# Third experts: VectorE in written order, routing of the last block and the second list in parts, block totals ahead of a tile's own work

## The chip, the cores and the metric

The kernel runs on one core of one Trainium2 chip. The metric is the device time of one execution in microseconds (us), the median of three runs: 3441.6 us (3441.32 to 3441.97).

Engine names in the profile: PE is TensorE's matrix products, PEld its weight loads, DVE is VectorE, ACT is ScalarE, POOL is GpSimd, SP is SyncE, which here issues most transfers.

## The reference, cut to what matters

The program is a network of four stages on 4096 tokens of 256 channels. The first three (two convolution-like attentions, and a linear attention with a first layer of experts) are not touched by the change. The last stage is a full attention over all 4096 tokens, and then a layer of eight experts, of which each token uses two:

```python
# layer 3 (t: 4096 tokens x 256 channels, float32)
t = t + attention(layer_norm(t))
xf = layer_norm(t)
gate_logits = xf @ Wg + bg                      # 8 experts
top_w, top_i = top_k(gate_logits, 2); top_w = softmax(top_w)
for e in range(8):
    h = gelu(xf @ W1[e] + b1[e])                # 256 -> 1024
    out = out + w_dense[:, e] * (h @ W2[e] + b2[e])   # 1024 -> 256
t = t + out
x = channels_first(t)
```

## The kernel before

**Tokens and blocks.** The 4096 tokens are held as 32 tiles of 128 tokens (`NT`), in eight blocks of 512 (`NBLK`, four tiles `TPB` each). The attention goes block by block. While it works on the values of block b, the tokens of block b - 1 are finished (`finish`, L2769: projection, division by the softmax sum, addition to `t`) and routed.

**Routing (`route_parts`, L2034).** For a block: statistics and layer norm (`stats`, `root`, `scales`, `norm`), two turns into channel-first form (`turn`), the gate's logits, the two best experts (`top`, whose Exp runs on ScalarE, then `weigh`), a running count per expert (`count`), places in the experts' lists (`place` on TensorE, `find` on VectorE) and `scatter`: eight indirect DMAs that GpSimd issues, each writing 128 token rows of 260 numbers into the DRAM table `xs`. `route` (L2023) groups these parts into five steps. All of them that need PSUM take it through `bank()`, which after the attention is a single bank named "q".

**Lists of tiles (`list_tiles`, L2120).** The experts' work is cut into tiles of 256 token rows of one expert (`MT`). A table says for each tile its expert and where its rows begin. List "A" has `FULL` = 20 tiles that are already full from blocks 0 to 6, so it is made during the attention of the last block; list "B" holds what is left (19 tiles, of which the last three lie inside a run-time branch, L2326, that tests how many are used). `list_tiles` is a generator of two parts: many small VectorE operations, then a product that spreads the table over partitions.

**Expert tiles (`expert_tiles`, L2329).** Tile numbers run from 0 to 35. For tile i the loop does, in this order of text: SP loads the rows of tile i + 4 (`expert_rows`, L2269) and the weights of tile i + 2 (two transfers, L2276 and L2278; three sets of buffers); `first` (L2360): eight groups of products with gelu on ScalarE (L2367), PSUM pairs in three buffers; `sides` (L2388, L2396): four weight differences on GpSimd; `turn` of the rows of tile i + 1 (L2298: four transposes, one VectorE copy, L2302); `where` for tile i + 1 (L2281: eight or nine tiny VectorE operations that work out target rows and gate weights); then `second` for the tile before, i - 1. `second` calls `seven` (L2399): the second layer in seven products of 2x2 blocks instead of eight, which needs four half sums `hs` of `h` on VectorE (L2403 to L2406), the weight differences, and a combining of the products (L2420 to L2425); then bias (L2431), scaling by the gate weight on ScalarE (L2438) and two indirect DMAs on GpSimd that write the result rows to the DRAM table `ys` (L2439).

**The last block's routing and list B** are put between these tiles: `step()` in `expert_tiles` calls one of five routing steps and then the two parts of list B, one or two per tile, in tiles 0 to 3. The four `finish` of the last block come ahead of tile 0 and after each of its first three pairs of products (`ahead`).

**Block totals.** A block of 512 tokens can be summed when no later tile holds one of its rows. `read(b)` (L2859) loads the two result rows of each token from `ys` (two transfers, L2496); `give(b)` (L2863) adds both to `t` on VectorE (L2867, 128 x 1024 each), turns the block with transposes (L251) into PSUM bank "q", copies it out, the first half on ScalarE (L254), the second on VectorE (L256), and `send` writes it to the output. Blocks 0 to 5 are read in tiles 29 to 34, each beside `second`, and given one tile later; block 6 is read after tile 35's `first`, ahead of the last `second`; block 7 after the branch. Blocks 6 and 7 are summed by TensorE during their transposes, after everything else. A read of `ys` waits for the result scatters that stand before it in the text, and a scatter that stands after it waits for the read.

**What sets the order.** By default a planner orders each engine's instructions by estimates of costs and of when inputs are ready. Inside `tc.manual_schedule(engines=...)` the named engines keep the order of the text. Before the change, the experts have TensorE in written order only until the last `step` (tile 3); VectorE, ScalarE, GpSimd and SP are the planner's. In the attention loop of the last blocks TensorE and GpSimd are in written order. `limits3` (L2895) tests for the attention's number range with some nine small VectorE operations; its result is used at the very end.

Of the kernel before, what the change touches and what calls it, by code (L numbers as in the profile page):

```python
# [19 lines left out]
P = 128  # L20
# [72 lines left out]
class Net:  # L93
# [2026 lines left out]
    def list_tiles(self, S, wp, bank, nm, n):  # L2120
# [25 lines left out]
        nc.vector.tensor_sub(new, have, had)  # L2146
        ends = tl(NBLK * NE, "ends")[:, :K]
# [8 lines left out]
        if not whole:  # L2156
            nc.vector.tensor_copy(S["used"], ends[:, K - 1 : K])
            last = tl(1, "last")
            nc.vector.tensor_scalar_add(last, ends[:, K - 1 : K], -1.0)
            i = tl(1, "i")  # L2160
            nc.vector.tensor_tensor(i, self.nth[:, 0:1], last, ALU.min)
        at = tl(1, "pair")
# [5 lines left out]
        nc.vector.tensor_mul(pick, pick, had)  # L2168
        k = tl(1, "k")
# [135 lines left out]
    def experts(self, S, steps=None, pre=None):  # L2305

        tc = self.tc
        early = steps is not None
# [4 lines left out]
        def some(tiles, steps=(), pre=None):  # L2313
            with (
# [3 lines left out]
            ):  # L2318
                if pre:
                    order.enter_context(tc.manual_schedule(engines={mybir.EngineType.PE}))  # L2320
                self.expert_tiles(S, tiles, wp, ps, list(steps), early, pre, order)

        some(tiles, steps or (), pre)
# [5 lines left out]
    def expert_tiles(self, S, order, wp, ps, steps, early, pre, written):  # L2329
# [25 lines left out]

        def turn(x):
# [3 lines left out]
        def first(xT, w1, between=None):  # L2360
# [8 lines left out]
            for m in range(0, KH, 2):  # L2369
                p = ps.tile([P, 2, MT], F32, tag="h", name="f_h_ps", bufs=3)  # L2370
                if between is None:
# [3 lines left out]
                else:  # L2375
                    products(m, p)
                    products(m + 1, p)
                    gelu(m, p)
                    gelu(m + 1, p)
                    for f in between[m // 2 : m // 2 + 1]:  # L2380
                        f()
# [17 lines left out]
        def seven(h, w2, wt, y):  # L2399

            hs = wp.tile([P, 4, KH // 2, P], F32, tag="hs", name="f_hs", bufs=2)
            a = h.rearrange("p (i m) (j n) -> p i m j n", i=2, n=P)
            nc.vector.tensor_tensor(hs[:, 0], a[:, 0, :, 1], a[:, 1, :, 1], ALU.add)  # L2403
            nc.vector.tensor_tensor(hs[:, 1], hs[:, 0], a[:, 0, :, 0], ALU.subtract)
            nc.vector.tensor_tensor(hs[:, 2], a[:, 0, :, 0], a[:, 0, :, 1], ALU.subtract)
            nc.vector.tensor_tensor(hs[:, 3], a[:, 1, :, 0], hs[:, 1], ALU.subtract)  # L2406
# [20 lines left out]
        def second(i, h, w2, wt, at, wgt):  # L2427
            y = wp.tile([P, NI, C], F32, tag="y", name="f_y")
            if L == 3:
                seven(h, w2, wt, y)  # L2430
# [13 lines left out]
        def step():  # L2444
            if steps:
                steps.pop(0)()
                if not steps:
                    written.close()

        nc.scalar.activation(wp.tile([P, 1], F32, tag="g", name="f_gelu", bufs=1), self.one, AF.Gelu)  # L2450
        beside, after = pre["beside"] if pre else ({}, {})
        xs, ws = {}, {}
        for i in tiles[:ahead_x]:
# [4 lines left out]
            if i not in xs:  # L2458
                xs[i] = rows(i)
        if pre:  # L2460
            pre["ahead"][0]()
            xT, to = pre["xT"], pre["to"]
        else:
            xT = turn(xs[tiles[0]])
            to = where(tiles[0], xs[tiles[0]])
        done = None
        for i in tiles:
# [5 lines left out]
            xs.pop(i)  # L2473
            h = first(xT, w1, (pre["ahead"][1:] if i == 0 else ()) if steps else None)
            now = (i, h, w2, sides(w2)) + to
            step()
            if i < tiles[-1]:
                xT = turn(xs[i + 1])
                to = where(i + 1, xs[i + 1])
            for f in beside.get(i, ()):  # L2480
                f()
            if done is not None:
                second(*done)
                step()
            for f in after.get(i, ()):
                f()
            done = now
        for f in beside.get(len(tiles), ()):
            f()
# [656 lines left out]
```

## Time and profile before

| | |
|---|---|
| median of three runs | 3441.6 us |
| the profiled execution's own time | 3443.34 us |
| its span, first to last instruction | 3441.2 us |
| mean granted TensorE clock | 0.950 |
| PE busy | 3117.4 us (91%) |
| DVE busy | 2317.2 us (67%) |
| POOL busy | 1466.2 us (43%) |
| ACT busy | 1330.2 us (39%) |
| third experts, first products to the last scatter's landing | about 2863 to 3423 us of the span |

Lines of the timeline give: start in us from the span's start, duration in us, engine, source line, operation, output<-input with shapes, how many are merged (x), and in brackets how long the engine had been idle and what ended that. "SPq" is a transfer that SP issues. Where a row has several engines' busy times, the order is PE, PEld, DVE, ACT, POOL, then granted clock (1.00 is full), DMA share and GB/s.

### The profile page before, as it was taken

The numbers are of one execution on the slowest core, as the hardware profiler recorded it, in microseconds if no ns is written. First come the engines' busy times: TensorE is split into PE (matmuls) and PEld (weight loads), VectorE is DVE, ScalarE is ACT, GpSimd is POOL, SyncE is SP. The second block draws the span as 40 slices with busy tenths as digits, with TensorE's granted clock in tenths as the row PEclk, the third lists the DMA queues.
The fourth block names the chain that finished last, engine by engine and source line by source line (L and its number), as shares of the span: only waits on it lengthen the run. The fifth ranks groups of instructions, "written<-read, shape, count | busy, mean of one in ns | idle before, by whom it ended". The sixth has DMA issues, their size and how long they took to land. (4 is left out here: it accounts for less than half of the span.)

```text
span 3441.2 us, 66030 instructions
## 1 busy us (share of the span) xinstructions
PE 3117.4 (91%) x25682; PEld 2333.0 (68%) x25682; DVE 2317.2 (67%) x5338; ACT 1330.2 (39%) x2552; POOL 1466.2 (43%) x1316
## 2 busy tenths in 40 slices
PE   6779999999977999897959789999999998999996
PEld 3443444344445888666748567888888887899986
DVE  8886777577754677796646576777777776555553
ACT  4444344433425665243434353222222223233331
POOL 2028788778834555343444353000000013555552
PEclk9889999999988999998769899999999999999998
DMA  1145656421143222100139663223333224555564
GB/s 71 43 118 141 169 155 168 120 65 52 49 127 100 71 71 78 38 1 3 50 133 286 205 219 119 94 88 99 98 99 104 80 93 163 184 202 215 196 219 143
DMA packets 241689, 407.01 MB, mean 118 GB/s; under 512 B 78354, under 2 KB 152851, under 8 KB 231891
## 3 DMA queue, kind: packets, MB, share of 16 engines
q1 hardware_dynamic: 212866, 347.55, 32.7%
q0 software_dynamic: 13056, 35.93, 2.8%
q10 hardware_dynamic: 15440, 19.16, 1.7%
q8 instruction: 207, 3.39, 0.4%
q14 instruction: 120, 0.98, 0.1%
HBM read 287.07 MB, written 111.30 MB: 116 GB/s over the span
## 5 line engine op out<-in xcount | busy, mean ns | idle before, releaser
L776 ACT COPY l_sc<-l_s 128x384 f32<-128x384 f32 (+1 forms) x632 | 303.9, 532 | 452.5 <-PE l_s L769 443.3
L152 PE MATMUL f_h_ps<-f_xT,f_w 128*128 128x256 f32 x1440 | 348.9, 393 | 23.6 <-ACT f_h L2367 17.8
L781 DVE TENSOR_TENSOR l_sm<-l_s,mask 128x256 f32<-128x256 f32 (+2 forms) x628 | 308.1, 551 | 89.0 <-PE l_s L769 87.7
L2112 POOL DMA_INDIRECT xs<-f_room,f_to x64 | 64.5, 1008 | 645.1 <-DVE a_e L2708 477.7
L152 PEld LDWEIGHTS f_h_ps<-f_xT,f_w 128*128 128x128 f32 x1440 | 268.1, 195 | 82.2 <-ACT f_h L2367 25.3
L769 PE MATMUL l_s<-l_q,l_k 32*128 32x256 f32 (+3 forms) x2944 | 270.9, 453 | 0.0
L2740 ACT ACTIVATE a_e<-a_e 128x512 f32<-128x512 f32 x256 | 156.0, 629 | 252.8 <-DVE a_e L2710 232.9
L786 POOL TENSOR_TENSOR l_sm<-l_sc,mask 128x768 f32<-128x768 f32 (+1 forms) x116 | 202.1, 1751 | 87.8 <-ACT l_sc L776 87.7
L2367 ACT ACTIVATE f_h<-f_h_ps,f_w 128x256 f32<-128x256 f32 x360 | 165.3, 470 | 192.0 <-PE f_h_ps L152 165.5
L1156 DVE TENSOR_TENSOR l_pr<-l_vk,l_w_ps 128x1280 f32<-128x1280 f32 x128 | 186.6, 1482 | 52.9 <-PE l_acc_ps L1160 34.3
L2439 POOL DMA_INDIRECT ys<-f_y,f_at x144 | 150.1, 1042 | 148.1 <-ACT f_y L2438 110.1
L769 PEld LDWEIGHTS l_s<-l_q,l_k 32*128 32x128 f32 x2944 | 132.7, 183 | 115.3 <-issue 67.5
L1160 PE MATMUL l_acc_ps<-ident,l_pr 128*128 128x128 f32 x1600 | 197.1, 277 | 6.5 <-POOL l_pr L1151 6.2
L1160 PEld LDWEIGHTS l_acc_ps<-ident,l_pr 128*128 128x128 f32 x1600 | 183.7, 143 | 13.3 <-POOL l_pr L1151 8.3
L2396 POOL TENSOR_TENSOR f_wt<-f_w 128x512 f32<-128x512 f32 x72 | 90.9, 1282 | 237.7 <-PE f_ya_ps L152 205.7
L790 POOL TENSOR_TENSOR l_sm<-l_sc,mask 128x256 f32<-128x256 f32 (+1 forms) x220 | 185.2, 870 | 16.0 <-ACT l_sc L776 15.2
L2721 PE MATMUL a_sa_ps<-a_q,a_kt 128*128 128x256 f32 x512 | 156.5, 387 | 19.6 <-DVE a_u L2726 17.6
L2725 ACT COPY a_u<-a_sa_ps 128x256 f32<-128x256 f32 x128 | 47.6, 372 | 294.5 <-PE a_sa_ps L2721 289.2
L815 PE MATMUL l_b_ps<-l_sm,l_v 128*32 128x256 f32 (+2 forms) x2176 | 153.5, 372 | 0.0
L2721 PE MATMUL a_sa_ps<-a_qt,a_kt 128*128 128x256 f32 x512 | 152.8, 380 | 0.0
L786 POOL TENSOR_TENSOR l_sm<-l_sc,mask_c 128x768 f32<-128x768 f32 (+1 forms) x64 | 121.1, 1909 | 37.0 <-ACT l_sc L776 36.4
L2760 PE MATMUL a_ob_ps<-a_et,a_vs 128*128 128x256 f32 x512 | 132.5, 381 | 0.0
(620 smaller groups left out, 7314.1 us busy)
## 6 DMA issues: line engine op xcount, KB each, us to landing
a_kt<-a_kd SPq DMA_DIRECT2D x128, 512.0 KB
f_w<-in_f_w SPq DMA_DIRECT2D x36, 1152.0 KB
f_w<-in_f_w SPq DMA_DIRECT2D x36, 1028.0 KB
xs<-zero SPq DMA_DIRECT2D x8, 4160.0 KB
l_vk<-vt SPq DMA_DIRECT2D x180, 128.0 KB
f_x<-xs SPq DMA_DIRECT2D x72, 260.0 KB
f_w<-in_f_w SPq DMA_DIRECT2D x36, 384.0 KB
l_rcp<-l_recd SPq DMA_DIRECT2D x48, 256.0 KB
```

What stands on the lines that cost most here:

```text
L152: self.nc.tensor.matmul(out, lhsT, rhs, start=(i == 0), stop=(i == len(pairs) - 1))
L769: nc.tensor.matmul(s[pair, j][:, at : at + m, :], key(hp), qs[hp], start=(z == 0), stop=(z == len(pieces) - 1))
L776: nc.scalar.copy(sc[:, j], s[1, j])
L781: nc.vector.tensor_tensor(to(pair, j, kind, at), pick(s[pair, j], kind, which), mask, ALU.mult)
L786: nc.gpsimd.tensor_tensor(out[:, :, at, :], of[:, :, which, :], bc(mask, 1, 2), ALU.mult)
L790: nc.gpsimd.tensor_tensor(to(1, j, kind, at), pick(sc[:, j], kind, which), mask, ALU.mult)
L815: nc.tensor.matmul(out, pieces[z][1](hp), self.halves(sms[pair][:, j], wide)[:, of + skip * lo : of + skip * (hi - 1) + 1 : skip], start=n ...
L1156: nc.vector.tensor_tensor(pr, vk, bc(held["w"][:, j, dy], 3, D), ALU.mult)
L1160: nc.tensor.matmul(acc[:, m, j, :], pf[:, dx, m * P : (m + 1) * P], self.ident, is_transpose=True, start=(j == 0 and dy == 0 and dx == 0 a ...
L2367: nc.scalar.activation(h[:, m, :], p[:, m % 2, :], AF.Gelu, bias=w1[:, 2 * hidden + m : 2 * hidden + m + 1])
L2721: mm = lambda out, i, right: nc.tensor.matmul(out, A[i], right, start=True, stop=True)
L2740: nc.scalar.activation(e[:, i : i + 3 : 2], e[:, i : i + 3 : 2], AF.Exp, scale=1.0 / 16.0)
```

## The change

In the experts of the third stage, VectorE follows the text for all tiles that are not in the branch. TensorE and GpSimd do so too, until the last entry of a `plan` for a tile below `FULL` has been done, which is tile 11's; after that VectorE alone. The `plan` replaces `step`, `beside` and `after`: it maps (tile, slot) to functions. The slots of tile i are 0 to 3 (ahead of each pair of products), "hs" (after the first half sum), "turn" (after turning and `where` of the next tile) and "end" (after `second`).

The half sums are taken out of `seven` and stand right behind their own tile's products: one, then slot "hs", then the second, then the next tile's turn, then the other two, then `where`. Tile 1 is turned in slot 3 of tile 0.

The last block's routing is spread over tiles 0 to 5 by its parts; the scatter's first four DMAs come at the end of tile 4, the other four at the end of tile 5. `list_tiles` has five parts instead of two; list B's go to tiles 5 to 9, and list A's, in the attention loop, to three steps instead of two, with the loads for tile 0 one step later. `limits3` moves into tile 11.

`give` is split: `add(b)`, the two sums on VectorE, goes to slot "hs" of the tile after the read; `give(b)`, transposes and copies (both copies now on ScalarE) and the output, to the end of that tile. The read of block 6 now stands behind the last `second`.

The diff, cut to its core:

```diff
     def list_tiles(self, S, wp, bank, nm, n):
         nc.vector.tensor_sub(new, have, had)
+        yield
...
             nc.vector.tensor_tensor(i, self.nth[:, 0:1], last, ALU.min)
+        yield
...
         nc.vector.tensor_mul(pick, pick, had)
+        yield
...
                 if pre:
-                    order.enter_context(tc.manual_schedule(engines={mybir.EngineType.PE}))
+                    order.enter_context(tc.manual_schedule(engines={ET.PE, ET.DVE, ET.Pool}))
...
+        plan = dict(pre["plan"]) if pre else {}
+
+        def extra(i, slot):
+            for f in plan.pop((i, slot), ()):
+                f()
...
-        def seven(h, w2, wt, y):
+        def sums(h):
+            if L == 2:
+                return None, ()
             hs = wp.tile([P, 4, KH // 2, P], F32, tag="hs", name="f_hs", bufs=2)
             a = h.rearrange("p (i m) (j n) -> p i m j n", i=2, n=P)
+            op = nc.vector.tensor_tensor
+            return hs, (
+                lambda: op(hs[:, 2], a[:, 0, :, 0], a[:, 0, :, 1], ALU.subtract),
+                lambda: op(hs[:, 0], a[:, 0, :, 1], a[:, 1, :, 1], ALU.add),
+                lambda: op(hs[:, 1], hs[:, 0], a[:, 0, :, 0], ALU.subtract),
+                lambda: op(hs[:, 3], a[:, 1, :, 0], hs[:, 1], ALU.subtract),
+            )
+
+        def seven(h, hs, w2, wt, y):
...
         if pre:
-            pre["ahead"][0]()
-            xT, to = pre["xT"], pre["to"]
+            turned[0], to[0] = pre["xT"], pre["to"]
+            plan[0, 3] = plan[0, 3] + [lambda: turned.update({1: turn(xs[1])})]
...
-            h = first(xT, w1, (pre["ahead"][1:] if i == 0 else ()) if steps else None)
-            now = (i, h, w2, sides(w2)) + to
-            step()
+            h = first(i, turned.pop(i), w1, not free)
+            hs, add = sums(h)
+            now = (i, h, hs, w2, sides(w2)) + to.pop(i)
+            for f in add[:1]:
+                f()
+            extra(i, "hs")
+            for f in add[1:2]:
+                f()
             if i < tiles[-1]:
-                xT = turn(xs[i + 1])
-                to = where(i + 1, xs[i + 1])
-            for f in beside.get(i, ()):
-                f()
+                if i + 1 not in turned:
+                    turned[i + 1] = turn(xs[i + 1])
+                for f in add[2:]:
+                    f()
+                to[i + 1] = where(i + 1, xs[i + 1])
+                xs.pop(i)
+            else:
+                for f in add[2:]:
+                    f()
+            extra(i, "turn")
             if done is not None:
                 second(*done)
-                step()
-            for f in after.get(i, ()):
-                f()
+            extra(i, "end")
             done = now
-        for f in beside.get(len(tiles), ()):
-            f()
+            if not free and not any(k < pre["free"] for k, _ in plan):
+                free = True
+                written.close()
+                written.enter_context(self.tc.manual_schedule(engines={mybir.EngineType.DVE}))
         second(*done)
+        extra(len(tiles), "end")
...
                             if b == NBLK - 1 and j == TPB + 5:
                                 lists = self.list_tiles(S, keep, bank, "A", FULL)
+                            if b == NBLK - 1 and j in (TPB + 5, TPB + 6):
                                 next(lists)
-                            if b == NBLK - 1 and j == TPB + 6:
+                                next(lists)
+                            if b == NBLK - 1 and j == TPB + 7:
                                 next(lists)
...
+            for i in range(TPB):
+                put(0, i, lambda i=i: (finish(last, i), part["stats"]([i])))
+            put(1, "turn", part["root"])
+            put(2, "hs", part["scales"], part["norm"])
+            put(2, "turn", lambda: part["turn"](0))
+            put(2, "end", lambda: part["turn"](1))
+            put(3, "turn", part["logits"], part["top"], part["exp"])
+            put(3, "end", part["weigh"], part["count"])
+            put(4, "turn", part["place"], part["find"])
+            put(4, "end", lambda: part["scatter"](range(2)))
+            put(5, "end", lambda: part["scatter"](range(2, TPB)))
+            put(5, "turn", go)
+            put(6, "hs", go)
+            put(7, "hs", go)
+            put(8, "hs", go)
+            put(9, "turn", go)
+            put(11, "hs", limits)
...
-                self.to_channels(keep_ps, "q", part, o)
+                self.to_channels(keep_ps, "q", t[:, b * TPB : (b + 1) * TPB, :], o, on_act=True)
...
+                put(i, "end" if i == MOST else "turn", lambda b=b: read(b))
+                if i + 1 < MOST:
+                    put(i + 1, "hs", lambda b=b: add(b))
+                    put(i + 1, "end", lambda b=b: give(b))
-            self.experts(
-                S, [go] * 5 + [more] * 2,
-                {**pre, "ahead": [lambda i=i: finish(NBLK - 1, i) for i in range(TPB)], "beside": (beside, after)},
-            )
+            self.experts(S, {**pre, "plan": plan, "free": FULL})
```

## The prediction

> **What bounds the kernel now.** I took the busy table first (TensorE 91% of the span), then the third experts by stretches, then the timeline inside the bad stretches and its two ends. The stretches (us; busy and count of PE, weight loads, VectorE, ScalarE, GpSimd; granted clock; DMA share; GB/s):
>
> ```profile
> 2861.70:2945.00 83.30, 67.54 (x380) 59.56 (x380) 49.98 (x191) 25.91 (x54) 39.81 (x34) 0.88 0.49 175
> 2945.00:3295.00 350.00, 350.00 (x2376) 321.70 (x2375) 190.28 (x502) 122.78 (x281) 192.70 (x152) 1.00 0.57 204
> 3295.00:3413.50 118.50, 101.71 (x656) 91.33 (x654) 63.32 (x107) 32.09 (x74) 52.43 (x38) 0.94 0.53 185
> 3413.50:3441.20 27.70, 8.95 (x50) 7.96 (x48) 3.92 (x13) 2.34 (x5) 1.94 (x2) 0.71 0.37 127
> ```
>
> The 350 us in the middle are pure TensorE at full clock: nothing on VectorE can make them shorter. A tile there takes 13.62 us (its first products start at 3104.34, the next tile's at 3117.96): first products 6.93, turning the next rows 0.44, the seven products of the tile before 6.25. All that can be won lies in the first row, the third and the tail. From the timeline of the early tiles:
>
> ```profile
> 2878.82 0.68 DVE L2302 COPY f_xT<-f_x_ps 128x512 f32<-128x512 f32 x1
> ...
> 2879.59 5.89 PE L152 MATMUL f_h_ps<-f_xT,f_w 128*128 128x256 f32 x13 [4.66 <-issue]
> ...
> 2934.73 0.87 DVE L2284 TENSOR_SCALAR f_first<-f_x,f_exA 128x2 f32<-128x2 f32 x1 [8.85 <-DMA f_x<-xs]
> ...
> 2939.34 0.68 PE L152 MATMUL a_q_ps<-f_put,all_one 128*128 128x57 f32 x2 [5.65 <-DVE f_put L2190]
> ```
>
> Tile 1's turned rows were copied late, behind routing, limit checks and `where` of later tiles, so PE stood 4.66 us. Later VectorE stood 8.85 us at a `where` whose rows (tile 7) were far ahead of need and queued behind the scatter; the list's table, which TensorE has in written order, waited behind it. From the late tiles:
>
> ```profile
> 3297.19 1.94 DVE L2867 TENSOR_TENSOR t<-t,f_room 128x1024 f32<-128x1024 f32 x1 [4.51 <-DMA f_room<-ys]
> ...
> 3301.91 0.69 DVE L2431 TENSOR_TENSOR f_y<-f_y,f_w 128x512 f32<-128x512 f32 x1
> 3302.63 0.91 ACT L2438 ACTIVATE f_y<-f_y,f_wgt 128x256 f32<-128x256 f32 x2 [4.37 <-DVE f_y L2431]
> ...
> 3304.31 2.58 PE L152 MATMUL f_h_ps<-f_xT,f_w 128*128 128x256 f32 x8 [3.97 <-ACT f_h L2367]
> ```
>
> A block total stands before the combining of a finished tile, waits for its read, the scaling waits for the combining, the gelus queue behind the scaling on ScalarE, and PE runs out of PSUM. PE's table of waits for this stretch (us, times, longest) has it six times:
>
> ```profile
> PE f_h_ps L152 <- ACT f_h L2367: 16.8, 6, 4.1
> ```
>
> **The change, part by part.**
>
> *Early tiles.* From PE's 2863.42 to the first products of tile 6 (2968.18) are 104.8 us. The work in it: 6 x 6.93 + 6 x 0.44 + 5 x 6.25 = 75.5, three `finish` 3 x 0.87, two routing turns 0.88, logits 1.70, place 0.36, the list's two products 0.6; 81.7 in all. So 23.1 are lost: waits of 5.6, 4.7, 2.8 (of kind "issue", during the scatter), 1.2 and 1.0, together 15.3, and 7.8 by the lower clock. Turning tile 1 now comes in tile 0's last slot, right behind `finish`; limits3 (9 small VectorE operations, 2873.41 to 2878.76) goes to tile 11; `where` runs one tile ahead only; routing comes in parts over tiles 1 to 5. That takes 4.7, 5.6, the 1.2 (a `finish` behind a `where`) and most of the clock's loss, 6. I leave the 2.8 (two half scatters replace one whole), the 1.0 (gelu behind the Exp's table load) and 1.8 of clock. Gain **17.5**, between 8 (a new wait as long as the old 4.7 with its clock) and 23.1.
>
> What moved and who covers it: the scatter's 8 indirect DMAs (1.28 us apart) now stand in GpSimd's written order at the ends of tiles 4 and 5, each half 5.1 us beside 5.6 us of weight differences and 2.3 of result scatters: 13.0 of 13.62, so GpSimd falls behind by at most a few us against a whole tile of slack (the differences are used by the next tile's seven products). On SP the row loads of tiles 9 and 10 wait for the half scatters, and the weights of tiles 7 and 8 behind them, with over one tile in hand. The second list's some 33 operations of 0.14 to 0.28 us, 6 us, go over tiles 5 to 9, where VectorE is idle 46%. If any of that cover fails, it costs its own length once, not per tile.
>
> *Attention's end.* The first list takes two attention steps more; its product and the three prefetches (rows and weights of tile 0) come one step (6.5 us) later. Before, the rows' load waited until 2838.03 for a scatter anyway, so it is later by 1 to 2 us; weights landed at 2848.45 and are first used at 2863.42. 0, between -3 and +3: VectorE is still in the planner's order there.
>
> *Middle.* The steady order is already the written one (half sums, turned rows, half sums, `where`, combining). 0.
>
> *Late tiles.* From 3294.98 to seven products' end at 3413.41 are 118.4 us; work: 6 x 6.93 + 5 x 0.44 + 7 x 6.25 = 87.5, six blocks' transposes 6 x 0.87 = 5.2; 92.7. Lost 25.7: 16.8 of the row above and 8.9 of clock. The totals (12 operations, 1.2 to 2.06 us) now come after the first half sum of the next tile, some 5.4 us into it; reads landed 2.2 and 4.8 us into it. The combining no longer stands behind them. Six copies of 0.68 leave VectorE, six of 0.59 join ScalarE, which is busy 32 of 118 us. I keep 1 us a tile of loss: gain **19**, between 8 and 25.
>
> Two rules are weighed here. *Port:* a total takes 1.2 us alone and up to 2.06 beside GpSimd. The Trainium skill, "SBUF — State Buffer", section "SBUF: two separate sides", says that a VectorE operation with two SBUF inputs and a GpSimd operation exclude each other for their whole length. By the row, both totals are done at 5.4 + 3.9 = 9.3 us, and turned rows two copies later at 10.7, against 14.5 when PE wants them. By the rule each waits a whole GpSimd operation (up to 1.96) first: 5.4 + 6.3, turned rows at 13.1. Still in time; but the slack is 1.4 us, and beyond it PE waits six times. I take the row, and put the rule into the range. *Clock:* "TensorE: Matmul & The Clock Gate", Part 1, has the clock halved after an idle window of about 3.4 us and back after as much work, so a gap costs 1.7 more, and a shorter one nothing. By the trace, tile 1's first products took 10.0 us instead of 7.1 after 4.66 idle, and gaps of 2.9 to 3.3 us were followed by slow ones too. By the page four gaps would return 6.8 us of clock in all, and the sum would be near 3412; by the rows it is some 12.
>
> *Tail.*
>
> ```profile
> 3413.45 0.34 SPq L2496 DMA_DIRECT2D f_room<-ys  x1
> ...
> 3419.52 0.97 POOL L2439 DMA_INDIRECT ys<-f_y,f_at  x1 [8.52 <-SPq L2326]
> ...
> 3423.37 0.34 SPq L2496 DMA_DIRECT2D f_w<-ys  x1
> ...
> 3429.05 0.69 PE L251 MATMUL tr_ps<-ident,f_w 128*128 128x128 f32 x2 [4.17 <-DMA f_w<-ys]
> ```
>
> Block 6's read was issued ahead of the last tile's scatter, and that scatter waited for it (ready at 3417.1, started at 3419.52). Now the read stands behind the last tile, so the scatter is 2.4 us earlier, but block 6's read starts with its landing, and block 7's behind that. If the branch for three spare tiles lets no read pass until block 6 has landed (5.3 us, as SP's sequence before suggests), block 7 lands 3.4 later; its transposes, warm from block 6's, take 2.7 instead of 4.1. **+2**, between -2 and +5.
>
> Sum: -17.5 + 0 - 19 + 2 = -34.5. The profiled execution's span is 3441.2, its own time 3443.34 (2.1 around the span): 3408.8 for such a one. The median of the runs shown is 1.7 below that execution, so **3407**.
>
> **Rivals.**
> - *The late waits stay* (ScalarE is still in the planner's order; totals now block turned rows if a read is late). For: six reads on a busy queue; the port rule. Against: reads landed by 4.8 us. Late gain 4: 3422. Chance 0.17.
> - *The early waits are replaced* (VectorE at the weights of the top two waits for ScalarE's Exp; PE in written order waits for the one PSUM bank of routing). Early gain 6: 3418.6. 0.13.
> - *All idle time goes, and the tail gains:* -23 - 24 - 2: 3392 to 3397. 0.10.
> - *Nothing won, or slower.* One mechanism: transfers bind in the late tiles. Per tile 2.2 MB of weights, 0.26 of rows, 1.05 of read, 0.5 of output, 0.26 of scatter, 4.3 MB in 14.5 us: 296 GB/s; the most in the 20 us stretches that I read is 290 (2860 to 2880). If reads landed later than about 9 us into their tile, VectorE in written order would stand there and the turned rows with it; to eat the early gain it must cost 41 us in six tiles, 6.9 each (25.7 now, and 15.5), so reads about 15 us into the tile. Then 3442 and above, 3450 at 8.3 each. Chance 0.05 for this and a gain that comes to nothing. That the order is the planner's own already is true of the middle tiles only.
>
> **How the numbers follow.** Forecast 0.55, its own range 3400 to 3415. Below 3397 and above 3424 I leave about one in ten each: the range takes in the two partial rivals and most of the good one. A measurement tells 0.2% (6.9 us) from no change; faster by that 0.95, within 0.02, slower 0.03.
>
> **What would show it.** Tile 6's first products 17 us earlier after its own start, no PE wait over 2 us in the early tiles and clock near 1.0; late tiles of 14.5 to 15.5 us instead of 16 to 20; totals without a DMA wait in front; the tail some 30 us instead of 27.7. It is wrong if VectorE stands in front of a total or of turned rows, or if ScalarE's gelus again queue behind a scaling.

## The result and the profile after

The kernel after takes 3429.9 us (median of eight runs, 3424.4 to 3435.3) against 3441.1 for the kernel before beside it: a ratio of 0.9968, 95% interval 0.9957 to 0.9979. It is faster, by 11.2 us; the forecast was 34.5, and 3429.9 lies above its range of 3397 to 3424.

The profiled span is 3427.9 us. The stretches of the kernel after, cut where its own stages begin (us; busy and count of PE, weight loads, VectorE, ScalarE, GpSimd; granted clock; DMA share; GB/s): tiles 0 to 5, tiles 6 to 29, tile 30 to the last product, the tail.

```profile
2860.70:2947.70 87.00, 83.83 (x540) 77.12 (x539) 60.33 (x150) 31.61 (x70) 42.47 (x35) 0.98 0.54 198
2947.70:3300.20 352.50, 335.05 (x2213) 303.30 (x2212) 214.87 (x519) 108.62 (x264) 184.76 (x152) 0.99 0.53 195
3300.20:3400.40 100.20, 95.73 (x656) 86.53 (x654) 61.97 (x128) 35.99 (x81) 45.75 (x38) 1.00 0.61 218
3400.40:3427.90 27.50, 8.92 (x50) 7.65 (x48) 3.90 (x13) 2.08 (x4) 1.92 (x2) 0.70 0.36 129
```

In the second row PE is no longer busy for the whole stretch: 335 of 352.5 us. By the starts of the first products, span against span: attention's end 2.7 earlier, tiles 0 to 5 from 104.8 to 87.0 (-17.8), **tiles 6 to 29 from 326.8 to 352.5 (+25.7)**, tile 30 to the last product from 118.5 to 100.1 (-18.4), tail -0.1. The sum, -13.3, is the difference of the spans. So the two gains came, and a stage costed at nothing gave most of them back.

Where it goes is in the steps (a tile's step runs from its first products to the next tile's). Before, tiles 5 to 29 take 13.62 us each. After, tiles 7 and 8 take 15.5 and 14.9, tile 12 takes 23.1, and tiles 13 to 29 14.38 each. A steady tile after, in the timeline (start in us, duration in us, then engine, line and operation; in brackets the idle time before it and its releaser):

```profile
3113.33 4.50 PE L152 MATMUL f_h_ps<-f_xT,f_w 128*128 128x256 f32 x20
3113.59 0.29 DVE L2442 TENSOR_TENSOR f_y<-f_u,f_yb_ps 128x128 f32<-128x128 f32 x1 [2.22 <-PE f_yb_ps L152]
3113.79 0.28 DVE L2443 TENSOR_TENSOR f_u<-f_u,f_ya_ps 128x128 f32<-128x128 f32 x1
...
3115.22 1.74 DVE L2452 TENSOR_TENSOR f_y<-f_y,f_w 128x512 f32<-128x512 f32 x1
...
3116.99 0.91 ACT L2459 ACTIVATE f_y<-f_y,f_wgt 128x256 f32<-128x256 f32 x2 [1.25 <-DVE f_y L2452]
3117.81 1.19 ACT L2380 ACTIVATE f_h<-f_h_ps,f_w 128x256 f32<-128x256 f32 x3
...
3118.31 2.86 PE L152 MATMUL f_h_ps<-f_xT,f_w 128*128 128x256 f32 x12 [0.48 <-ACT f_h L2380]
```

The same place before:

```profile
3104.01 0.29 DVE L2422 TENSOR_TENSOR f_u<-f_u,f_ya_ps 128x128 f32<-128x128 f32 x1 [2.14 <-ACT f_u L2420]
...
3104.34 6.87 PE L152 MATMUL f_h_ps<-f_xT,f_w 128*128 128x256 f32 x31
3104.67 0.28 DVE L2421 TENSOR_TENSOR f_y<-f_u,f_yb_ps 128x128 f32<-128x128 f32 x1
...
3105.51 1.24 DVE L2431 TENSOR_TENSOR f_y<-f_y,f_w 128x512 f32<-128x512 f32 x1
...
3106.78 0.91 ACT L2438 ACTIVATE f_y<-f_y,f_wgt 128x256 f32<-128x256 f32 x2
```

The line numbers give it away: before, VectorE ran line 2422 ahead of line 2421. The text has `flat[:, 0]` first, which needs the last of the seven products; the planner had put `u2` first, whose inputs are ready 0.6 us sooner. In written order the chain waits for PE, and the bias add ends 3.6 us after the next tile's first product (3116.96 - 3113.33) instead of 2.4 (3106.75 - 3104.34): 0.7 us by its start, 0.5 because it runs longer beside GpSimd's weight differences, 1.74 us instead of 1.24. ScalarE stands 1.25 us at the scaling with the gelus behind it, and PE stops.

The rows of the late tiles and the tail, to hold against those shown of before: PE's wait table from tile 30 on, then three lines of the timeline.

```profile
PE f_h_ps L152 <- ACT f_h L2380: 4.5, 6, 0.8
```

```profile
3337.97 2.48 DVE L2918 TENSOR_TENSOR t<-t,f_room 128x1024 f32<-128x1024 f32 x2
...
3403.56 0.96 POOL L2460 DMA_INDIRECT ys<-f_y,f_at  x1 [4.94 <-ACT f_y L2459]
...
3417.94 0.46 PE L251 MATMUL tr_ps<-ident,f_w 128*128 128x128 f32 x2 [0.22 <-DMA f_w<-ys]
```

The late gelu wait is 4.5 us instead of 16.8, the totals (two in one row of 2.48 us) wait for no read, and the last scatter starts 3.2 us after the last product instead of 6.0.

### The profile page after: what moved, and what is told of

The parts are those of the page before. It is cut to its first block, busy times and chain, and to the rows that moved or that the text cites. A ratio compares the mean times of both kernels' runs of the same rounds, so it can differ in the third digit from the quotient of the medians.

```text
span 3427.9 us, 66058 instructions
## 1 busy us (share of the span) xinstructions
PE 3111.8 (91%) x25682; PEld 2327.6 (68%) x25682; DVE 2353.5 (69%) x5332; ACT 1327.0 (39%) x2558; POOL 1455.1 (42%) x1316
## 5 line engine op out<-in xcount | busy, mean ns | idle before, releaser
L786 POOL TENSOR_TENSOR l_sm<-l_sc,mask 128x768 f32<-128x768 f32 (+1 forms) x116 | 202.6, 1754 | 87.8 <-ACT l_sc L776 87.7
L2460 POOL DMA_INDIRECT ys<-f_y,f_at x144 | 142.3, 988 | 193.6 <-ACT f_y L2459 144.4
L2380 ACT ACTIVATE f_h<-f_h_ps,f_w 128x256 f32<-128x256 f32 x360 | 157.7, 469 | 164.0 <-PE f_h_ps L152 134.2
L1160 PEld LDWEIGHTS l_acc_ps<-ident,l_pr 128*128 128x128 f32 x1600 | 185.1, 144 | 12.9 <-POOL l_pr L1151 7.8
L2750 PE MATMUL a_sa_ps<-a_q,a_kt 128*128 128x256 f32 x512 | 156.9, 388 | 17.8 <-DVE a_u L2755 15.9
```

The costliest lines, as they stand in the source:

```text
L786: nc.gpsimd.tensor_tensor(out[:, :, at, :], of[:, :, which, :], bc(mask, 1, 2), ALU.mult)
L1160: nc.tensor.matmul(acc[:, m, j, :], pf[:, dx, m * P : (m + 1) * P], self.ident, is_transpose=True, start=(j == 0 and dy == 0 and dx == 0 a ...
L2380: nc.scalar.activation(h[:, m, :], p[:, m % 2, :], AF.Gelu, bias=w1[:, 2 * hidden + m : 2 * hidden + m + 1])
L2750: mm = lambda out, i, right: nc.tensor.matmul(out, A[i], right, start=True, stop=True)
```

## The experiments

All kernels in one table first; stages in us from each profile, so that the small differences in time between chips don't matter. "T0-5" is from tile 0's first products to tile 6's, "T30+" from tile 30's first products to the last product. The ratio is to the kernel before, timed beside it.

| kernel | T0-5 | T6-11 | T12 | T13-29 | T30+ | tail | span | ratio (95%) |
|---|---|---|---|---|---|---|---|---|
| before | 104.8 | 81.7 | 13.6 | 231.5 | 118.5 | 27.7 | 3441.2 | 1 |
| after | 87.0 | 85.0 | 23.1 | 244.4 | 100.1 | 27.6 | 3427.9 | 0.9968 (0.9957-0.9979) |
| swap | 86.5 | 85.9 | 20.9 | 231.5 | 95.7 | 27.3 | 3410.2 | 0.9901 (0.9884-0.9918) |
| pairs | 87.0 | 85.0 | 14.4 | 231.5 | 101.6 | 27.5 | 3410.5 | 0.9881 (0.9858-0.9904) |
| dvefree | 87.1 | 85.0 | 23.9 | 231.5 | 114.3 | 27.5 | 3437.1 | 0.9984 (0.9976-0.9991) |
| allwritten | 88.3 | 83.8 | 13.6 | 231.2 | 105.4 | 27.5 | 3419.4 | 0.9908 (0.9892-0.9925) |
| swappairs | 84.8 | 84.8 | 20.1 | 231.2 | 93.2 | 27.4 | 3405.3 | 0.9901 (0.9885-0.9918) |
| swapends | 84.9 | 92.4 | 13.6 | 231.5 | 95.7 | 26.9 | 3406.8 | 0.9920 (0.9903-0.9936) |
| addback | 87.7 | 84.8 | 21.8 | 231.5 | 112.2 | 28.3 | 3425.2 | 0.9965 (0.9954-0.9975) |
| peonly | 87.4 | 85.8 | 13.6 | 231.5 | 95.7 | 27.4 | 3403.9 | 0.9898 (0.9882-0.9915) |
| nopool | 81.7 | 82.8 | 13.6 | 231.5 | 95.7 | 28.0 | 3394.1 | 0.9858 (0.9833-0.9882) |
| lump | 87.0 | 81.6 | 20.9 | 231.5 | 95.7 | 27.2 | 3406.2 | 0.9894 (0.9869-0.9918) |
| lumpplan | 98.0 | 81.6 | 13.6 | 231.5 | 95.7 | 27.1 | 3412.4 | 0.9915 (0.9890-0.9941) |
| best1 | 84.0 | 87.8 | 13.6 | 231.2 | 93.2 | 27.7 | 3401.5 | 0.9875 (0.9848-0.9901) |

What the stages leave out, the start of tile 0, lies between 2858.9 and 2869.6 in the kernels that share all code up to there; before is at 2863.4. Two spans can thus differ by up to 10 us for that alone. Each stage comes from one profile, and the early ones scatter too: in tiles 0 to 5 the eight kernels that have the routing spread alike and three engines in written order (after to addback in the table) lie between 84.8 and 88.3.

### The order of the sums (swap)

```diff
-            nc.vector.tensor_tensor(flat[:, 0], u1, pb[:, 2], ALU.add)
             nc.vector.tensor_tensor(u2, u1, pa[:, 1], ALU.add)
             nc.vector.tensor_tensor(u, pa[:, 2:4], bc(u2, 1, 2), ALU.add)
+            nc.vector.tensor_tensor(flat[:, 0], u1, pb[:, 2], ALU.add)
```

> Edit: in the seven products' combining, the sums u2 and u stand ahead of the output flat[:, 0] again, as the planner issued them before. Theory A (the written order puts flat[:, 0] first, which needs pb's last product, so the whole combining chain, the bias add and ScalarE's two scalings end about 1.2 us later, and the scalings push a gelu past the point where TensorE needs its PSUM tile): the bias add ends about 2.4 us after the next tile's first product instead of 3.6, the step of tiles 12 to 29 falls from 14.37 to about 13.6 us (18 x 0.76 = 13.7 us), the stretch from tile 6's first products to tile 30's from 352.5 to about 338, and the time from about 3430 to 3412 to 3416. Theory B (VectorE and GpSimd are held up on their common port because the written order sets them side by side, whatever the order of the sums): the bias add stays at 1.7 us, the step stays within 0.15 us of 14.37, the time within 3 us of after's 3430. Theory C (any order that isn't the planner's costs): a gain of some 3 us.

Theory A holds: one line changed its place and the step is 13.62 us again. A steady tile of this kernel:

```profile
3164.38 0.29 DVE L2442 TENSOR_TENSOR f_u<-f_u,f_ya_ps 128x128 f32<-128x128 f32 x1 [1.43 <-ACT f_u L2441]
...
3164.72 7.09 PE L152 MATMUL f_h_ps<-f_xT,f_w 128*128 128x256 f32 x32
...
3165.89 1.24 DVE L2452 TENSOR_TENSOR f_y<-f_y,f_w 128x512 f32<-128x512 f32 x1
...
3167.16 0.91 ACT L2459 ACTIVATE f_y<-f_y,f_wgt 128x256 f32<-128x256 f32 x2
```

The bias add ends 2.41 us after the first product, as before the change, and PE does 32 products without a stop. The seventeen tiles gain 12.9 us, tile 12 2.2, the late tiles 4.5 (with a start of tile 0 that is 1.8 later, 0.3 more up to tile 12 and 0.3 less in the tail, the span falls by 17.7). VectorE and GpSimd still meet at the bias add (1.24, not the 0.69 that it takes in the late tiles of before), so theory B as the cause of the step falls; a part of the lateness, 0.5 of 1.2 us, is that meeting.

### Where the late scaling bites (pairs)

```diff
-            h = first(i, turned.pop(i), w1, not free)
+            h = first(i, turned.pop(i), w1, bool(pre))
```

> Edit: the first products of every tile are issued two by two ahead of their two gelus, as in tiles 0 to 11, so that TensorE has 24 products to run before it needs a gelu of the same tile, and not 20. Theory A: the combining chain stays late (bias add's end 3.6 us after the first product) but TensorE no longer waits for the gelu: the step of tiles 12 to 29 is about 13.6 us, the time 3412 to 3418. Theory B (port): the chain is as late, and since the same things collide TensorE's step follows VectorE's, 14.3 us: the time stays at 3427 to 3432. Theory C (a switch of TensorE and GpSimd back to the planner's order at tile 12 is what costs): the first steps after tile 12 stay long, above 14 us, since the switch is still there.

Here the combining stays in the bad order, and comes even later, because the planner now runs the next `where` ahead of it beside GpSimd. A steady tile:

```profile
3158.74 7.07 PE L152 MATMUL f_h_ps<-f_xT,f_w 128*128 128x256 f32 x32
3160.72 0.84 ACT L2380 ACTIVATE f_h<-f_h_ps,f_w 128x256 f32<-128x256 f32 x2 [2.35 <-PE f_h_ps L152]
...
3165.48 0.69 DVE L2452 TENSOR_TENSOR f_y<-f_y,f_w 128x512 f32<-128x512 f32 x1
...
3166.21 0.91 ACT L2459 ACTIVATE f_y<-f_y,f_wgt 128x256 f32<-128x256 f32 x2 [4.65 <-DVE f_y L2452]
```

The bias add ends 7.4 us after the first product, ScalarE stands 4.65 us, and PE doesn't notice: it needs two gelus to run all 32 products. In the kernel after, two groups of products share one PSUM buffer with a gelu between them, and after 20 products PE needs the third gelu (it starts again at the end of that gelu, to 0.05 us). The step needs both: a late chain and a PE that depends on the gelu behind it. The Trainium skill has a rule that would ask for this wait ("PSUM — Partial Sum Buffer", section "PSUM bank collisions raise a hardware error": access by two engines is to be guarded by the bank, not by the address); no run here tries it without the wait. The late stage of pairs, 101.6 us, holds one step of 21.9 us (tile 31) that is not explained.

### VectorE's order from tile 12 on (dvefree)

```diff
                 written.close()
-                written.enter_context(self.tc.manual_schedule(engines={mybir.EngineType.DVE}))
```

> Edit: VectorE too goes back to the planner's order from tile 12 on, so the rest of the change stands alone. Theory A: the order of the sums is the planner's again, the step of tiles 12 to 29 is 13.6 us (gain 13.7), and the late tiles get back the waits of before (tile 30's first products to tile 35's last ones 118 instead of 100 us, a loss of 18): the time is 3431 to 3438. Theory B (port): the step of tiles 12 to 29 stays at 14.3, since GpSimd's work is the same, and the late tiles lose 18 as well: 3445 to 3450. Theory C (VectorE's written order as such): as A in the middle.

The middle steps are 13.62 again, and the late waits come back: 114.3 us, near the 118.5 of before. The written order is thus needed in six tiles and harmful in seventeen, for one swapped line. Tile 12 keeps its long step (23.9), so VectorE's order there is not what makes it.

### Written order on three engines throughout (allwritten)

```diff
             if not free and not any(k < pre["free"] for k, _ in plan):
-                free = True
-                written.close()
-                written.enter_context(self.tc.manual_schedule(engines={mybir.EngineType.DVE}))
+                pass
```

> Edit: TensorE, VectorE and GpSimd keep the written order in all 36 tiles, and so the first products go two by two in all. Theory A: no stall at the change from tile 11 to 12 beyond the limits' own work (its step 23.1 falls by 6 to 9 us), the step of tiles 12 to 29 is about 13.6 us; the late tiles lose 1 us or so a tile where a block's turning stands in TensorE's written order behind ScalarE's copy: 3405 to 3412. Theory B (port): GpSimd's where and sides in written order collide as much or more: step 14.3 or above, 3427 to 3435. Theory C (the planner's return at tile 12 costs): gain only at tile 11 to 12, some 9 us, 3421.

Tile 12's extra 9.5 us are gone and the middle is at 13.60, as theory A said; the first products go two by two in all tiles here, as in pairs. The late tiles lose more than the 1 us a tile that it gave (105.4 us against 93.2 in swappairs and best1): in PE's wait table there, 4.3 us are for a block's copy out of the single PSUM bank "q" and 4.3 for gelus.

### Both mends (swappairs)

> Edit: both mends at once, the sums u2 and u ahead of flat[:, 0], and the first products two by two in every tile. Theory A (one cause: the late combining chain stops TensorE only where a gelu shares its PSUM tile with the next product): the two don't add up in tiles 12 to 29, whose step is 13.60 us as with either alone; the step from tile 11's first products to tile 12's, and from 12's to 13's, is 13.6 to 14.4 (20.9 with the first mend alone); the late tiles take 14.6 us a step: from tile 30's first products to the last ones 92 to 96 us; the time 3396 to 3405. Theory D (two separate causes that add up): the step of tiles 12 to 29 falls below 13.4 us.

The steps of tiles 13 to 29 are 13.60, the same as with either alone, so there is one cause and not two. The late tiles are as expected, 93.2. The expectation for tile 12 missed: 20.1 us, where pairs alone had 14.4. In pairs ScalarE runs two gelus before it stands at tile 12's late scaling (6.76 us); here the planner has the scaling after only one, and PE stops for 4.5 us after 24 products. So that mend hides the long step of tile 12 or doesn't, by where the planner puts the scaling; the cause of the step lies elsewhere.

### The limits, or the change of order (swapends)

```diff
-            put(11, "hs", limits)
...
-                    self.attn3(t, S, out, lambda: self.limits3(S, mpool))
+                    self.attn3(t, S, out, None)
+                    self.limits3(S, mpool)
```

> Edit, on the kernel with the sums in the former order: the checks of the limits go back behind the experts, where they were before the change, so that tile 11 carries no extra work and the written order of TensorE and GpSimd ends two tiles earlier, after tile 9. Theory E (the long step at tile 12, 20.9 us, comes from the change from the written to the planner's order: GpSimd does the sides of tile 11 late and those of tile 12 early, and VectorE's small operations for the rows run beside them at 1.2 us each): the long step moves to tile 10 or 11, 18 to 21 us. Theory F (it comes from the limits' operations on VectorE in tile 11): no step from 9 to 14 is above 15 us, and the time falls by 6 to 7. The tail (from the last product to the end) under the prediction's step: 2 us longer if the limits had stood in its way, as long as before (27.3) if not.

The long step moves with the end of the written order: tile 10 takes 20.7 us and tile 12 13.6. Theory E holds, F falls. Whether TensorE's change of order or GpSimd's makes the step, the next run tells. The tail is 26.9 us against 27.3, so the limits had not made it longer or shorter by more than 0.4.

### GpSimd alone (nopool)

```diff
-                    order.enter_context(tc.manual_schedule(engines={ET.PE, ET.DVE, ET.Pool}))
+                    order.enter_context(tc.manual_schedule(engines={ET.PE, ET.DVE}))
```

> Edit, on the kernel with the sums in the former order: GpSimd is never in written order in the experts; TensorE (to tile 11) and VectorE (to the end) as in that kernel. Theory E (GpSimd's change of order at the end of the plan makes the one long step): no step after tile 9 is above 15 us, tile 12's is 13.6 instead of 20.9; from tile 12's first products to tile 30's 245.1 us instead of 252.4; time 3402 to 3405. Rival (TensorE's change, which comes at the same place, makes it): tile 12's step stays at 18 to 21 us. In the early tiles, by theory: 84 to 88 us to tile 6, since the parts are placed as before; if GpSimd's written order is what keeps the sides and the scatters apart there, the steps of tiles 4 to 6 grow by 2 to 4 us each.

It is GpSimd. Tile 12's step is 13.6 us, and the early stage fell to 81.7, which no theory had. Tile 12 in the kernel after, where the long step is:

```profile
3030.19 1.61 POOL L2408 TENSOR_TENSOR f_wt<-f_w,f_wt 128x512 f32<-128x512 f32 x1
...
3032.27 1.23 DVE L2290 TENSOR_SCALAR f_first<-f_x,f_exA 128x2 f32<-128x2 f32 x1
...
3034.66 2.49 POOL L2408 TENSOR_TENSOR f_wt<-f_w 128x512 f32<-128x512 f32 x2
3034.75 1.19 DVE L2292 TENSOR_TENSOR f_wgt<-f_second,f_x 128x2 f32<-128x2 f32 x1
3035.97 1.20 DVE L2293 TENSOR_SCALAR f_second<-f_second 128x2 f32<-128x2 f32 x1
...
3042.30 0.91 ACT L2459 ACTIVATE f_y<-f_y,f_wgt 128x256 f32<-128x256 f32 x2 [7.17 <-DVE f_y L2452]
...
3043.61 5.49 PE L152 MATMUL f_h_ps<-f_xT,f_w 128*128 128x256 f32 x12 [6.39 <-ACT f_h L2380]
```

The sides of tile 11 come late by the written order and those of tile 12 at once by the planner's, eight operations in a row (3028.8 to 3039.7). VectorE's `where`, 0.2 us an operation elsewhere, takes 1.2 beside them, the combining follows it, then the scaling, then PE's 6.4 us, and 12 products at half the clock (5.49 instead of 2.86 us; granted clock 0.50 from 3044 to 3048).

Why the sides are late in written order is in GpSimd's table of waits from the first products to 3050, in swap and in nopool:

```profile
POOL ys L2460 <- ACT f_y L2459: 62.8, 10, 10.7
```

```profile
POOL f_wt L2408 <- PE f_ya_ps L152: 54.8, 10, 7.4
```

In the text, tile i's sides stand behind the result scatter of tile i - 2, and that scatter waits for the scaling. With written order GpSimd stands at the scatter (62.8 us in all) and does the sides 6 to 13 us into the tile (tiles 2 and 8 of the kernel after); by the planner it starts them 0.7 us before the tile does (tile 2 of nopool), and waits only for their buffer. Late sides meet whatever VectorE has then. In tile 2 it is the routing's layer norm, and PE, whose next instruction is the turn of those rows, stands three times. After, then nopool:

```profile
2890.09 5.98 DVE L240 TENSOR_SCALAR f_room<-t,ln_mv,ln_rstd 128x256 f32<-128x256 f32 x4
...
2893.59 0.33 PE L2060 MATMUL a_q_ps<-ident,f_room 128*128 128x128 f32 x1 [1.00 <-DVE f_room L240]
...
2896.40 1.92 PE L152 MATMUL f_ya_ps<-f_w,f_h 128*128 128x128 f32 x8
```

```profile
2890.35 1.43 DVE L240 TENSOR_SCALAR f_room<-t,ln_mv,ln_rstd 128x256 f32<-128x256 f32 x4
```

GpSimd's written order cost 4.7 us in tiles 0 to 5, 3.1 in tiles 6 to 11 and 7.3 in tile 12 (swap against nopool, one profile each). The first figure is the loosest: tile 2's step is 14.5 us in nopool and 17.6 to 21.1 in the eight kernels named under the table. It is not bad everywhere: allwritten has it in all tiles with steps of 13.60 in tiles 12 to 29. This kernel differs from the one after by two edits, and its ratio is 0.9858 (0.9833 to 0.9882): faster than before and than after (0.9968).

### Totals ahead of a tile's own (addback)

```diff
-                    put(i + 1, "hs", lambda b=b: add(b))
-                    put(i + 1, "end", lambda b=b: give(b))
+                    put(i + 1, "end", lambda b=b: (add(b), give(b)))
```

> Edit, on the kernel with the sums in the former order: a block's two additions go back behind the tile's own combining, right ahead of the block's turning. The prediction's step for the late tiles (both parts are needed: VectorE's written order, and the totals early): the late step rises from 15.03 by 2 to 3 us, since TensorE comes to the block's turning some 2.5 us before the additions of 1.24 us each are through; from tile 30's first products to the last ones 105 to 112 us instead of 95.7; time 3420 to 3427. Rival (VectorE's order alone does it, as the run with VectorE free from tile 12 suggests with 114 us): the late step stays at 15.0 to 15.5 and the time at 3410.

112.2 us instead of 95.7. Four of the six pairs of totals now run beside GpSimd's sides and take 4.5 us instead of 2.5. PE's wait table has one new row, for the totals:

```profile
PE tr_ps L251 <- DVE t L2918: 13.8, 5, 4.0
```

So the late gain needs both parts, VectorE's written order (dvefree) and the place of the totals (this run): either alone leaves 112 to 114.

### What freed the early tiles (peonly, lump, lumpplan)

peonly takes VectorE and GpSimd out of the written order of tiles 0 to 11 (`engines={ET.PE}`). lump keeps the written order and puts routing and list back into the steps of before; lumpplan does both. The lines that lump adds (those of the spread parts go):

```diff
+            put(0, "hs", lambda: (part["stats"](range(TPB)), part["root"](), part["scales"](), part["norm"]()))
+            put(1, "hs", lambda: part["turn"](0))
+            put(1, "end", lambda: part["turn"](1))
+            put(2, "hs", lambda: (part["logits"](), part["top"](), part["exp"](), part["weigh"](), part["count"]()))
+            put(2, "end", lambda: (part["place"](), part["find"](), part["scatter"](range(TPB))))
+            put(3, "hs", go, go, go, go)
+            put(3, "end", go)
```

> Edit, on the kernel with the sums in the former order: in tiles 0 to 11 only TensorE keeps the written order (as before the change); VectorE and GpSimd go by the planner's, and from tile 12 on all is as in that kernel. The prediction's step for the early tiles (the planner's order of VectorE made TensorE wait; VectorE's written order takes that away): from the first products to tile 6's 98 to 106 us instead of 86.5; time 3420 to 3430. Rival (the cutting of the routing and of the list into parts does it, in whatever order VectorE takes them): 86 to 90 us, time 3410 to 3414.

> Edit, on the kernel with the sums in the former order: the last block's routing and list B are put back into the five and two steps in which the kernel before had them (statistics to norm in tile 0, the turns in tile 1, logits to the whole scatter in tile 2, the list in tile 3), while VectorE, TensorE and GpSimd keep the written order of the early tiles. The prediction's step (VectorE's written order, the turn of tile 1 and the limits moved are what frees TensorE; the cutting is only what makes that possible at a small cost): from the first products to tile 6's 86 to 92 us. Rival (the spreading over tiles 1 to 9 is what frees it, whatever the order): 98 to 108 us, time 3422 to 3432.

> Edit: the same lumps as in the run before this one, with VectorE and GpSimd in the planner's order in tiles 0 to 11, which leaves of the change's early part only the earlier turn of tile 1, the limits in tile 11 and the routing's three generator steps for list A. The spreading as cause: from the first products to tile 6's 100 to 105 us (104.8 before the change), time 3416 to 3421. The turn of tile 1 and the limits' move as cause (the 4.7 us wait in tile 1 and its clock): 94 to 99 us.

Spread parts in the planner's order: 87.4 (and no long step at tile 12, since GpSimd's order doesn't change there). Lumps in written order: 87.0. Lumps in the planner's order: 98.0, where PE still stands 7.0 us for the list's table. So neither rival is right alone: either the order or the spreading brings most of the gain. With all three engines in written order the two together bring no more (86.5, swap), but that is GpSimd's doing. Peonly and nopool differ in VectorE's order alone, and there it is worth 5.7 us beside the spreading in tiles 0 to 5 (87.4 against 81.7) and 3.0 in tiles 6 to 11 (85.8 against 82.8). What it takes away can be seen in tile 5 of peonly: the bias add runs into GpSimd's sides and takes 4.70 us, the scaling waits for it, and PE stands 1.97 us for a gelu.

What lumpplan keeps of the change up to tile 6 (the earlier turn of tile 1, the limits moved, the first list in three steps) gives 6.8 of the 17.8 us. Lump also has 81.6 in tiles 6 to 11, where swap has 85.9 and nopool 82.8, so the spreading is what costs there, and mostly with GpSimd in written order: list parts in tiles 6 to 8 that meet its late sides.

### All mends (best1)

The sums, pairs, GpSimd free, list parts of tiles 6 to 8 moved to "turn", and the two turns of the routing half a tile later.

> Edit, all mends together: the sums in the former order, first products two by two everywhere, GpSimd never in written order, the list parts of tiles 6 to 8 behind the next tile's turn instead of behind the first half sum, and the routing's two turns half a tile later (end of tile 2, first slot of tile 3) than its norm. By the steps of the single runs: from tile 12's first products to tile 30's 244.8 us; late 93.2; the step of tiles 7 and 8 13.6 to 14.0 each instead of 14.8 (gain 2); tile 2's step 14 to 15 instead of 17.6 to 19 (gain 3 to 4). Time 3394 to 3399. If the mends stand in each other's way (the planner's GpSimd runs its sides beside the parts that were moved): 3402 to 3406.

The middle and the late tiles are as expected, but tile 3 takes 18.1 and tile 10 18.6 us: 3401.5 us of span against nopool's 3394.1, of which 3.2 lie ahead of tile 0. By their ratios the two are not told apart; what the run shows is that the mends together win nothing over nopool. Tile 10 shows tile 12's pattern again (`where` beside GpSimd's sides at 1.2 us an operation, then a gelu wait of 3.1 us). There the moved parts, or the pairs, shifted what meets what; which of them is not settled. Tile 3 has no wait over 0.35 us: the later of the two turns now stands right ahead of the logits' sixteen short products (128x8), and of the products behind them eight take 1.91 us, at a granted clock of 0.50 from 2914 to 2916.

## Why the prediction was right and wrong

- **Early tiles, -17.5: measured -17.8.** The size was right, in part by luck. The waits named are gone, but either part of the change alone would have taken most of them. I left 5.6 us of loss (the scatter, the Exp's table, clock), and none of these came; the kernel after has 5.3 above the 81.7 us of work, all in tile 2, by GpSimd's order. nopool reaches 81.7 with PE busy throughout, so the sum of the work was right to a tenth.
- **"GpSimd falls behind by at most a few us against a whole tile of slack": failed.** I counted its busy time and asked whether TensorE needs the sides in time. TensorE never waited for them. I did not name the instruction that GpSimd would stand at in written order, the result scatter behind ScalarE's scaling, nor what a late side does to VectorE: 15.1 us in tiles 0 to 12. That price stood in the trace of before, in the very wait that I put down to routing, limits and `where`:

```profile
2876.06 2.61 POOL L2396 TENSOR_TENSOR f_wt<-f_w,f_wt 128x512 f32<-128x512 f32 x2
2876.15 1.19 DVE L2285 TENSOR_SCALAR f_second<-f_first 128x2 f32<-128x2 f32 x1
```

- **Attention's end, 0: measured -2.7**, inside the spread of kernels with the same code there.
- **"Middle. The steady order is already the written one ... 0": this is the step that failed, by 25.7 us.** I compared the order of the groups and not the lines within the combining, and I put the whole stage at nothing though GpSimd's order changes in it too. The timeline showed the lines out of order, 2422 ahead of 2421, and PE's slack was readable: in before as in swap the third gelu ends 0.6 us before PE needs it. 12.9 of the 25.7 are the order of the sums in tiles 13 to 29; 9.5 are tile 12, where GpSimd changes order, 2.2 of it by the sums as well; 3.3 come in tiles 6 to 11, with list parts and late sides. "Nothing on VectorE can make them shorter" was true, and said nothing on longer.
- **"If any of that cover fails, it costs its own length once":** a lateness of 1.2 us in a steady tile costs 0.76 seventeen times.
- **Late tiles, -19: measured -18.4.** Right in size and mechanism, and shown by dvefree and addback. The step is 15.78 us where I gave 14.5 to 15.5; 0.75 of it is the sums again, and the rest goes with pairs (14.55).
- **Port rule or row:** the totals took 1.22 us each (1218 to 1226 ns), the row; the rule's case did not come in the kernel after. In addback it does: two totals beside GpSimd took 4.49 us. What decided was such a meeting elsewhere, on operations that I had at their bare price.
- **Clock rule or rows:** after 6.39 us idle 12 products took 5.49 us instead of 2.86, as both say. In tile 2 the clock fell after waits of 1 us, so the rule as I read it, that a short gap costs nothing, did not hold there.
- **Tail, +2: measured -0.1.** The mechanism is as put: the scatter comes 2.8 us earlier after the last product, block 7's read lands 2.0 later (17.6 against 15.6 us), where I had 3.4, and its transposes take 2.8 us instead of 4.1, as I had it. The last copy and output, which I had not counted, end 0.8 sooner.

Of the rivals, none came: late waits fell from 16.8 to 4.5 us, the early ones were replaced by 2.9 us in tile 2 alone, and "slower, by transfers" found no support, as no total waits for a read. One sign that I had named did come, ScalarE's gelus behind a scaling, but in the middle tiles, where I had put nothing.

## What to carry to other kernels

When an engine is taken from a planner's order to the order of the text, list the engine's instructions of one steady iteration by line number, in the order of the trace: every place where the numbers fall is a place where the text will run differently, and its price, if it has one, comes once per iteration. Then name, for every engine put in written order, the instruction at which it will stand longest and what stands behind it; an engine with slack of its own can still be late in a way that hurts a third one. Switching an engine's order in the middle of a loop is an edit of its own, with the late work of one order and the early work of the other in the same tile.

## What the hardware showed that I had not expected

VectorE operations on two numbers per partition, with one tensor as input (line 2293), take 1.2 us beside GpSimd's tensor operations and 0.17 alone (tile 12 and tile 11 of the kernel after), and the layer norm's four scalings 5.98 against 1.43 (tile 2, after and nopool). I had put the port rule on operations with two SBUF inputs only. That it is the port and not something else that the two engines share is argued from the lengths, which match GpSimd's 1.23 to 1.3 us an operation, and not shown.

TensorE's clock fell without a long gap: in tile 2 of the kernel after, three waits of 0.94 to 1.00 us with one transposition of 0.33 between them were followed by eight products in 1.92 us, against 1.06 in nopool; the granted clock was 0.50 from 2896 to 2898. One gap of 3.4 us, as I had read the rule, was not needed here. In tile 3 of best1 there was one wait of 0.35 us, within some 3 us of transpositions and short products, and it fell too (0.50 from 2914 to 2916). How little work it takes, no run tells.
